# Identity transposes ahead of the first rows, and every projection one piece earlier, in a local-attention and mixture-of-experts kernel

## The chip, the cores and the metric

The kernel runs on one core of a Trainium2 chip. The time is the device time of one launch in microseconds (us); each kernel is launched several times, and the median is compared. In the code, `nc.tensor` is TensorE (PE: matrix products and transposes), `nc.vector` is VectorE (DVE), `nc.scalar` is ScalarE (ACT), `nc.gpsimd` is GpSimd (POOL), and `nc.sync` is the queue that issues the DMAs (SP).

## The reference

The input `x` has 2 sequences of 2048 rows of 256 numbers. An attention layer with 16 heads of 16, in which each row looks at itself and the 64 rows before it, is followed by a layer norm, a router that picks one of 8 experts for each row, the expert's first layer with GELU, a shared second layer, and two layer norms.

```python
qkv = x @ W_attn + b_attn
scores = jnp.einsum('bhtd,bhsd->bhts', q, k) * scale
scores = jnp.where(mask[None, None], scores, -jnp.inf)   # causal & (j >= i - 64)
attn = jax.nn.softmax(scores, axis=-1)
out = jnp.einsum('bhts,bhsd->bhtd', attn, v) ... @ W_proj + b_proj
x = _layernorm(x + out)
router_logits = x @ Wr.T
expert_idx = argmax(softmax(router_logits))
inter = gelu(x @ W1[e] + b1[e])          # e: the row's expert
y = inter @ Wo + bo + x
x = _layernorm(x + (layernorm(y) * gamma + beta))
```

## The kernel before

Everything is in 32-bit floats, apart from the masks. The 4096 rows are 32 tiles of 128 rows (`NT`), and 8 chunks of 512 rows (`CH`; 4 tiles each, `TPC`).

**Start.** SP issues the loads of the first chunk, of the bias rows `bst`, of the weights `wa` in three parts (for q, k and v) and the rest. POOL builds `ident`. PE transposes the biases into `pb` (L288) and DVE copies them to `bqkv` (L289) and scales them into `bq1` (L315); then DVE builds the masks `m_a`, `m_b` and `m_first` in some twenty small operations (L331 to L356). This part is ordered by a scheduler; from L938 on, the order of each engine's queue is the order in which the code is written.

**Projections of a chunk.** They are cut into four pieces of two parts each: piece 0 transposes the chunk's rows (L368) into `xT`, piece 1 makes q (L372), piece 2 makes k (L372), piece 3 makes v (L379). `project` issues the PE work of one part, `keep` the copies out of PSUM by ACT and DVE, `prepare` takes the buffers (and issues the load of the next chunk with piece 0, POOL's copy of 64 old columns of k with piece 2, POOL's clearing of v with piece 3). PSUM tiles of the projections come from a ring of two banks (`psum`), those of the transposes from another ring of two (`ps_t`), the scores have four banks of their own. After piece 3, DMAs shift v by 64 rows into `h` (L456 to L463). Pieces 0 to 2 of chunk 0 run ahead of the loop (L947).

**The loop over tiles** (L1000) is a hand-written software pipeline. Iteration i computes the scores of tile t = i (`scores`: masks L474, products L486), the row maxima on DVE (`row_max`, L498) and the exponentials on ACT (`exps`, L502) in four quarters, and POOL's partial sums (`fold`, L514 and L522); turns the probabilities of tile u = i-1 (`turn`, L552; copies by ACT L558 and DVE L560) and multiplies them by v (`weigh`, L572); normalises and projects tile w = i-2 (`turn_inverse` L591, `normalise` L595, `join` L603); and does the layer norm of tile z = i-3 (`norm_scale` on POOL L619 and L620, `norm` on DVE L628, `turn_x1` L641, `keep_x1` L646). Between these, iteration i does piece i % 4 of chunk i // 4 + 1. After piece 2, POOL adds the bias to the residual of the chunk (`add_bias`, L943). With i % 4 = 2 there is the router's product (`route`, L653), with i % 4 = 3 its transposition (`turn_logits`, L663, then DVE L664), once at i = 8 that of the expert biases (`turn_biases`, L933). From i = 20 on, DVE and POOL also build the lists of the rows of each expert (POOL `row` L788, i = 25 to 28). Iterations 28 to 31 have no piece.

In iteration 0, after the first quarter's maxima, the code turns the router's weights (`turn_router`, L296), makes v of chunk 0 (piece 3), and adds the bias to chunk 0's residual; the other three quarters' maxima follow on DVE. v's two additions of the bias (L446) are then ahead of them in DVE's queue.

**The experts** follow: 36 blocks of 128 gathered rows (up to 39 if the routing needs them), each a first layer (L188), GELUs (L197) and a second layer (L206).

Of the kernel before, what the change touches and what calls it, by code (L numbers as in the profile page):

```python
# [10 lines left out]
F32 = mybir.dt.float32  # L11
# [3 lines left out]
ALU = mybir.AluOpType  # L15
AX = mybir.AxisListType

P = 128
# [3 lines left out]
TPC = CH // P  # L22
NEG = -1.0e30
GAP = 64
SPLIT = (0, 16, 28, 32)
PIECES = 8
EARLY = 1
LN_EPS_BLOCK = 1e-5
LN_EPS_FFN = 1e-12
# [3 lines left out]
def kernel(  # L33
# [16 lines left out]
    nc = tc.nc  # L50
    B, T, C = x.shape
    E, _, FF = w1.shape
    KC = C // P
# [56 lines left out]
    def psum(name):  # L110
        return ps_m.tile([P, 512], F32, tag="pm", name=name)
# [136 lines left out]
    with ExitStack() as att:  # L248
# [34 lines left out]
            nc.sync.dma_start(out=bp_bc, in_=b_proj.partition_broadcast(P))  # L283


        bqkv = aw.tile([P, 3 * KC], F32, name="bqkv")
        pb = psum("pb")
        nc.tensor.transpose(pb[:, 0 : 3 * KC], bst, ident[0 : 3 * KC, 0 : 3 * KC])  # L288
        nc.vector.tensor_copy(bqkv, pb[:, 0 : 3 * KC])  # L289

        nc.gpsimd.memset(wrT, 0.0)

        def turn_router():
            pw = psum("pw")
            for k in range(KC):
                nc.tensor.transpose(pw[:, ts(k, E)], wrs[:, ts(k, P)], ident[0:E, 0:E])  # L296
            nc.vector.tensor_copy(
                wrT[:, :, 0:E], pw[:, 0 : KC * E].rearrange("p (k e) -> p k e", e=E)
            )
# [10 lines left out]
        unit = HD**-0.5 / HD  # L310
        nc.vector.tensor_scalar(half[:, 0:1], par_f, -unit, HD**-0.5, ALU.mult, ALU.add)
        nc.vector.tensor_scalar(half[:, 1:2], par_f, unit, None, ALU.mult)

        bq1 = aw.tile([P, KC], F32, name="bq1")
        nc.vector.tensor_scalar(bq1, bqkv[:, 0:KC], half[:, 1:2], None, ALU.mult)  # L315

# [35 lines left out]
        m_first = aw.tile([P, 4, P], BF16, name="m_first")  # L355
        nc.vector.tensor_copy(m_first, off.unsqueeze(1).to_broadcast([P, 4, P]))  # L356
        m_first = m_first.rearrange("p h c -> p (h c)")

        qs, ks, vs, vh, xbs, axT, x1s, x1Ts, pxs = {}, {}, {}, {}, {}, {}, {}, {}, {}
        pts, banks, probs, maxes, sums, pTs, pas, rTs, avs, norms = [{} for _ in range(10)]  # L360
# [2 lines left out]
        def project(c, piece, part):  # L363

            pm = psum(f"pj_{c}_{piece}_{part}")
            if piece == 0:
                for j in range(TPC):
                    nc.tensor.transpose(pm[:, ts(j, P)], xts[c][:, j, ts(part, P)], ident)  # L368
            elif piece in (1, 2):
                f = (piece - 1) * KC + part  # L370
                for k in range(KC):
                    nc.tensor.matmul(  # L372
                        pm, lhsT=wa[:, k, ts(f, P)], rhs=axT[c][:, k, :],
                        start=(k == 0), stop=(k == KC - 1),
                    )
            else:
                for a in range(2):
                    for k in range(KC):
                        nc.tensor.matmul(  # L379
                            pm[:, ts(a, C)],  # L380
                            lhsT=axT[c][:, k, ts(2 * part + a, P)],
                            rhs=wa[:, k, 2 * C : 3 * C],
                            start=(k == 0), stop=(k == KC - 1),
                        )
            pxs[c, piece, part] = pm

        def prepare(c, piece):

            first = c % (TPB // TPC) == 0
            if piece == 0:  # L390
                if c + 1 < B * T // CH:
                    xts[c + 1] = load_x(c + 1)
                axT[c] = p2.tile([P, KC, CH], F32, tag="xT", name=f"xT_{c}", bufs=1)
                xbs[c] = xp.tile([P, TPC, C], F32, tag="xb", name=f"xb_{c}")
            elif piece == 1:
                qs[c] = p2.tile([P, KC, 2, CH], F32, tag="q", name=f"q_{c}")
            elif piece == 2:
                ks[c] = p2.tile([P, KC, CTX + CH], F32, tag="k", name=f"k_{c}")
                if first:
                    nc.gpsimd.memset(ks[c][:, :, 0:CTX], 0.0)  # L400
                else:
                    nc.gpsimd.tensor_copy(ks[c][:, :, 0:CTX], ks[c - 1][:, :, CH : CH + CTX])
            else:

                vs[c] = p2.tile([P, TPC, NH // 2, 3, HD], F32, tag="v", name=f"v_{c}")
                nc.gpsimd.memset(vs[c][:, :, :, 1, :].rearrange("p j m d -> p (j m) d"), 0.0)

                vh[c] = p2.tile([P, TPC, NH // 2, 3, HD], F32, tag="h", name=f"h_{c}")
                if first:
                    nc.gpsimd.memset(vh[c][0:CTX, 0].rearrange("p m s d -> p (m s d)"), 0.0)  # L410
# [273 lines left out]
        def routing_constants():  # L684
            e_rank = iota([P, E], [[-1, E]], E, 0, "e_rank")[1]
            e_gap = iota([P, E], [[GAP, E]], 0, 0, "e_gap")[1]
            col = iota([P, P], [[1, P]], 0, 0, "col")
            own = iota([P, 1], [[0, 1]], 0, 1, "own")[1]
            tile1 = iota([P, NT], [[1, NT]], 1, 0, "tile1")[1]
            before = rt.tile([P, P], BF16, name="before")  # L690
            nc.gpsimd.memset(before, 1.0)
            nc.gpsimd.affine_select(
                out=before, in_=before, pattern=[[1, P]], compare_op=ALU.is_gt,
                fill=0.0, base=0, channel_multiplier=-1,
            )
            ones = rt.tile([P, P], BF16, name="ones")
            nc.gpsimd.memset(ones, 1.0)
            one_e = rt.tile([P, E], F32, name="one_e")
            nc.gpsimd.memset(one_e, 1.0)
            none = rt.tile([P, E], F32, name="none")  # L700
            nc.gpsimd.memset(none, 0.0)
            carry[-1] = none
            for n, (t0, t1) in enumerate(lots):
                pads[n] = rt.tile([P, t1 - t0 + 1, E], BF16, name=f"oh_{n}")
                nc.gpsimd.memset(pads[n][:, t1 - t0, :], 0.0)
            return e_rank, col, own, before, ones, one_e, tile1, e_gap
# [293 lines left out]
        for i in range(NT):  # L1000


            t, u, w, z = (n if n >= 0 else None for n in range(i, i - 4, -1))
            c, piece = i // TPC + 1, i % TPC
            more = c < NT // TPC
            if more:
                prepare(c, piece)
            if w is not None:
                inverse(w)
            scores(t)  # L1010
            row_max(t, 0)
            if i == 0:
                consts = routing_constants()
                turn_router()
                prepare(0, 3)
                for part in range(2):
                    project(0, 3, part)
                    keep(0, 3, part)
                add_bias(0)
            if u is not None:  # L1020
                turn(u, 0)
                keep_turned(u, 0)
                turn(u, 1)
            exps(t, 0)
            row_max(t, 1)
            if u is not None:
                keep_turned(u, 1)
            if z is not None:
                norm_scale(z)
            if more:  # L1030
                project(c, piece, 0)
            exps(t, 1)
            row_max(t, 2)
            row_max(t, 3)
            if t < NT - 1:
                fold(t, 0)
            for task in spread.get(i, ()):
                task()
            if u is not None:
                turn(u, 2)  # L1040
                keep_turned(u, 2)
                turn(u, 3)
                keep_turned(u, 3)
            if more:
                keep(c, piece, 0)
            if z is not None:
                norm(z)
            exps(t, 2)
            if more:
                project(c, piece, 1)  # L1050
            if w is not None:
                turn_inverse(w)
                normalise(w)
            if more:
                keep(c, piece, 1)
            if u is not None:
                weigh(u)
            exps(t, 3)
            if t < NT - 1:
                fold(t, 1)  # L1060
            if u is not None:
                keep_weighed(u)
            if z is not None:
                turn_x1(z)
                keep_x1(z)

            if i == TPC:
                load_experts()
            if i == 2 * TPC:
                turn_biases()  # L1070
            if i >= TPC + 3 and (i - 3) % TPC == 0:
                turn_logits((i - 3) // TPC - 1)
            for task in plan.get(i, ()):
                task()
            if w is not None:
                join(w)
            if more and piece == 2:
                add_bias(c)
            if z is not None and z % TPC == TPC - 1:
                route(z // TPC)  # L1080
# [178 lines left out]
```

## Time and profile before

| What | us |
|---|---|
| median of 3 runs (639.22 to 640.71) | 639.62 |
| the profiled execution's own time | 637.24 |
| its span, first to last instruction | 635.5 |

The loop's iterations can be read from the start of the mask products (L474) of each tile in PE's timeline:

| Iterations | start, us | length, us |
|---|---|---|
| 0 | 18.95 | scores of tile 1 begin at 26.48 and are complete only after 30.7 |
| 2 (piece 2), 3 (piece 3) | 40.52, 49.92 | 9.40, 9.71 |
| 4 (piece 0), 5 (piece 1) | 59.63, 67.99 | 8.36, 9.49 |
| 6 (piece 2, router), 7 (piece 3, logits) | 77.48, 87.55 | 10.07, 10.17 |
| 8 (piece 0, expert biases), 9 (piece 1) | 97.72, 106.86 | 9.14, 9.50 |
| 24, 25, 26, 27 (pieces 0 to 3, lists) | 251.91, 260.27, 269.76, 280.39 | 8.36, 9.49, 10.63, 10.85 |
| 28, 29, 30 (no piece) | 291.24, 299.54, 307.95 | 8.30, 8.41, 9.86 |

The profile's page gives each engine's busy share, the span in 40 slices, and the chain of work that ended last. The timeline gives instructions in order of time; a line begins with the start and the duration in us, then the engine and the line of the code, and ends, in brackets, with the time that the engine sat idle before it and what released it. A merged line's duration reaches from the first start to the last end. The view of windows gives each engine's busy time in a stretch, then the TensorE clock granted (1.00 is full), the DMA share and the rate.

### The profile page before, as it was taken

To read this page: it belongs to the slowest core of one execution; us is meant where nothing else is said; L and a number is where in the kernel's file an instruction comes from. 1 tells how busy PE (TensorE), PEld (TensorE's weight loads), DVE (VectorE), ACT (ScalarE), POOL (GpSimd) and SP (SyncE) were. 2 spreads that over 40 slices of the span, in tenths; PEclk is the share of its full clock that TensorE was granted. 3 is DMA by queue.
4 is the path that set the end of the run, shared out by engine and by line. 5 is a ranking of instruction groups with operands and counts; after the bars stand their busy time and mean duration, and the time that the engine had idled before them with its cause. 6 is when DMAs were issued, how large, how long until landed. Compare 5 with 4: busy or idle time off the path is not lost.

```text
span 635.5 us, 18444 instructions
## 1 busy us (share of the span) xinstructions
PE 575.8 (91%) x7334; PEld 467.6 (74%) x7335; DVE 382.3 (60%) x904; ACT 299.1 (47%) x997; POOL 429.0 (68%) x628
## 2 busy tenths in 40 slices
PE   5899999999999999998777993899999999999990
PEld 3467676676767767676556993799999999999990
DVE  4468877788687887988783355444434444334442
ACT  1365775766676674865743331133343333333330
POOL 4158676676867678789743487377777777777752
PEclk9889999999999999999998997799999999999995
DMA  4202503030030302004233454155555555565300
GB/s 152 74 3 51 155 9 103 19 93 20 28 79 19 101 11 67 20 11 119 78 96 131 150 168 157 50 192 183 162 172 183 205 177 163 170 186 198 119 19 16
DMA packets 34708, 65.31 MB, mean 103 GB/s; under 512 B 8555, under 2 KB 22970, under 8 KB 34620
## 3 DMA queue, kind: packets, MB, share of 16 engines
q1 hardware_dynamic: 31164, 55.19, 26.6%
q0 software_dynamic: 3456, 8.92, 5.9%
q8 instruction: 59, 0.97, 0.7%
q14 instruction: 29, 0.24, 0.1%
HBM read 49.46 MB, written 8.91 MB: 92 GB/s over the span
## 4 chain that ended last, share of the span: by engine, by line
PE 70%; POOL 11%; DVE 7%; ACT 7%; issue 4%; POOLq 0%; DVEq 0%; ACTq 0%
PE ph L188 18%; PE py L206 17%; PE pj L372 8%; ACT pr L502 5%; PE pt L552 5%; PE py L603 4%; PE pa L572 4%; PE s L486 4%; PE pj L379 3%; PE s L474 2%; POOL row L788 2%; POOL fd L522 1%; POOL fd L514 1%; PE px L641 1%; PE pr L591 1%
## 5 line engine op out<-in xcount | busy, mean ns | idle before, releaser
L197 ACT ACTIVATE gT<-ph,bc 128x128 f32<-128x128 f32 x288 | 82.4, 369 | 183.9 <-issue 155.2
L502 ACT ACTIVATE pr<-s,nm 128x128 f32<-128x128 f32 x512 | 140.7, 409 | 8.5 <-DVE nm L498 8.5
L188 PEld LDWEIGHTS ph<-xgT,wb 128*128 128x128 f32 x1152 | 134.4, 192 | 5.0 <-ACT xgT L174 1.6
L188 PE MATMUL ph<-xgT,wb 128*128 128x128 f32 x1152 | 135.2, 275 | 2.4 <-ACT xgT L174 1.3
L514 POOL TENSOR_TENSOR fd<-pr 128x512 f32<-128x512 f32 x62 | 78.7, 1271 | 78.5 <-ACT pr L502 78.4
L206 PE MATMUL py<-wo_sb,gT 128*128 128x256 f32 x576 | 131.6, 382 | 0.0
L206 PEld LDWEIGHTS py<-wo_sb,gT 128*128 128x128 f32 x576 | 107.7, 192 | 13.4
L498 DVE TENSOR_REDUCE nm<-s 128x4 f32<-128x512 f32 x128 | 82.0, 683 | 11.2 <-PE s L486 10.9
L522 POOL TENSOR_TENSOR fd<-fd 128x512 f32<-128x512 f32 (+2 forms) x93 | 76.4, 822 | 7.3
L558 ACT COPY pT<-pt 128x512 f32<-128x512 f32 x64 | 38.2, 597 | 86.0 <-DVE nm L498 53.3
L552 PE MATMUL pt<-ident,pr 128*128 128x128 f32 x512 | 71.9, 281 | 2.0 <-ACT pT L558 1.8
L552 PEld LDWEIGHTS pt<-ident,pr 128*128 128x128 f32 x512 | 57.0, 142 | 19.8 <-issue 12.5
L235 DVE TENSOR_SCALAR res<-y,mv_c,rs_c 128x256 f32<-128x256 f32 x36 | 14.9, 413 | 83.9 <-POOL rs_c L220 83.9
L372 PE MATMUL pj<-xT,wa 128*128 128x512 f32 x128 | 63.5, 625 | 1.6 <-issue 1.6
L560 DVE COPY pT<-pt 128x512 f32<-128x512 f32 x64 | 43.8, 684 | 14.3 <-PE pt L552 14.3
L219 POOL TENSOR_TENSOR rs_b<-mv_b,eps_ffn 128x1 f32<-128x1 f32 x36 | 16.0, 445 | 45.9 <-DVE mv_b L217 45.9
L486 PEld LDWEIGHTS s<-k,q 32*64 32x64 f32 x2048 | 31.5, 133 | 14.6 <-issue 14.6
L237 POOL DMA_INDIRECT out_dram<-res,s_idx_b x27 | 27.8, 1031 | 20.0 <-DVE res L235 20.0
L486 PE MATMUL s<-k,q 32*64 32x128 f32 x2048 | 39.4, 283 | 0.0
L372 PEld LDWEIGHTS pj<-xT,wa 128*128 128x128 f32 x128 | 23.4, 202 | 21.2 <-issue 20.4
L603 PE MATMUL py<-wpj,av 128*128 128x256 f32 x128 | 35.3, 399 | 2.8 <-DVE logits L664 2.1
L129 POOL DMA_INDIRECT xg<-x_d,g_idx_b x27 | 33.4, 1237 | 5.2 <-issue 5.2
(183 smaller groups left out, 830.7 us busy)
## 6 DMA issues: line engine op xcount, KB each, us to landing
wb<-in_L_ffn_W_dram SPq DMA_DIRECT2D x33, 1024.0 KB, 5.1
xt<-in_L_attn_x_dram SPq DMA_DIRECT2D x8, 512.0 KB, 5.9
x_d<-x SPq DMA_DIRECT2D x32, 128.0 KB, 1.7
h<-v SPq DMA_DIRECT2D x8, 384.0 KB, 4.5
wb<-in_L_ffn_W_dram SPq DMA_DIRECT2D x24, 128.0 KB, 2.2
h<-v SPq DMA_DIRECT2D x8, 288.0 KB, 3.3
wo_sb<-in_L_ffn_Wo_dram SPq DMA_DIRECT2D x1, 1024.0 KB, 7.0
wa<-in_L_attn_W_attn_dram SPq DMA_DIRECT2D x3, 256.0 KB, 4.5
```

The lines of the kernel that those rows point to most:

```text
L188: nc.tensor.matmul(phs[b, h][:, f % (NF // 2), :], lhsT=wb[:, k, ts(f, P)], rhs=xT[:, k, :], start=(k == 0), stop=(k == KC - 1),)
L197: nc.scalar.activation(gT[:, f, :], ph[:, f % (NF // 2), :], AF.Gelu, bias=bcs[b][:, f : f + 1], scale=1.0,)
L206: nc.tensor.matmul(py[:, 0:C], lhsT=gT[:, f, :], rhs=wo_sb[:, f, :], start=(f == 0), stop=(f == NF - 1),)
L372: nc.tensor.matmul(pm, lhsT=wa[:, k, ts(f, P)], rhs=axT[c][:, k, :], start=(k == 0), stop=(k == KC - 1),)
L486: nc.tensor.matmul(banks[i][r][a * CTX : (a + 1) * CTX, 2 * g + o, :], lhsT=qs[c][rows, g, o, t0 : t0 + CTX], rhs=ks[c][rows, g, t0 : t0 + P],
L498: nc.vector.tensor_reduce(maxes[i][:, r, :], banks[i][r], AX.X, ALU.max, negate=True)
L502: nc.scalar.activation(probs[i][:, r, x, :], banks[i][r][:, x, :], AF.Exp, bias=maxes[i][:, r, x : x + 1], scale=1.0,)
L514: nc.gpsimd.tensor_tensor(fd[:, 8 * pair : 8 * pair + 8, :], pr[:, two, :, 0:CTX].rearrange("p r x c -> p (r x) c"), pr[:, two, :, CTX:P]. ...
L522: nc.gpsimd.tensor_tensor(fd[:, :, 0:n], fd[:, :, 0:n], fd[:, :, n : 2 * n], ALU.add)
L552: nc.tensor.transpose(pt[:, x, :], probs[i][:, r, x, :], ident)
L560: nc.vector.tensor_copy(pTs[i][:, r], pt)
L603: nc.tensor.matmul(py[:, 0:C], lhsT=av[:, k, :], rhs=wpj[:, k, :], start=(k == 0), stop=(k == KC - 1),)
```

## The change

Three things. First, 16 transposes of `ident` by `ident` are issued on PE ahead of everything else, into a PSUM tile that nobody reads, and the biases' transposition with its two DVE operations is written after the masks. Secondly, iteration 0 takes all four quarters' maxima before v's biases. Thirdly, the loop does piece (i + 1) % 4 of chunk (i + 1) // 4 + 1, so that piece 0 of chunk 1 and its piece 1 both fall into iteration 0, and iteration 27 has no piece; `add_bias` follows piece 3 instead of piece 2, which is the same iteration as before; `turn_router` moves to iteration 3.

```diff
+WARM = 16
-        bqkv = aw.tile([P, 3 * KC], F32, name="bqkv")
-        pb = psum("pb")
-        nc.tensor.transpose(pb[:, 0 : 3 * KC], bst, ident[0 : 3 * KC, 0 : 3 * KC])
-        nc.vector.tensor_copy(bqkv, pb[:, 0 : 3 * KC])
...
-        bq1 = aw.tile([P, KC], F32, name="bq1")
-        nc.vector.tensor_scalar(bq1, bqkv[:, 0:KC], half[:, 1:2], None, ALU.mult)
...
         m_first = m_first.rearrange("p h c -> p (h c)")
+        pw = psum("warm")
+        for n in range(WARM):
+            nc.tensor.transpose(pw[:, 0:P], ident, ident)
+        bqkv = aw.tile([P, 3 * KC], F32, name="bqkv")
+        pb = psum("pb")
+        nc.tensor.transpose(pb[:, 0 : 3 * KC], bst, ident[0 : 3 * KC, 0 : 3 * KC])
+        nc.vector.tensor_copy(bqkv, pb[:, 0 : 3 * KC])
+        bq1 = aw.tile([P, KC], F32, name="bq1")
+        nc.vector.tensor_scalar(bq1, bqkv[:, 0:KC], half[:, 1:2], None, ALU.mult)
...
-            c, piece = i // TPC + 1, i % TPC
+            c, piece = (i + 1) // TPC + 1, (i + 1) % TPC
...
             row_max(t, 0)
             if i == 0:
                 consts = routing_constants()
+                for r in range(1, 4):
+                    row_max(t, r)
+                for r in range(2):
+                    exps(t, r)
+                prepare(0, 3)
+                prepare(1, 0)
+                for n in ((0, 3), (1, 0)):
+                    for part in range(2):
+                        project(*n, part)
+                        keep(*n, part)
+                add_bias(0)
+                for r in range(2, 4):
+                    exps(t, r)
+                for part in range(2):
+                    project(c, piece, part)
+                    keep(c, piece, part)
+                for pair in range(2):
+                    fold(t, pair)
+                continue
+            if i == 3:
                 turn_router()
-                prepare(0, 3)
-                for part in range(2):
-                    project(0, 3, part)
-                    keep(0, 3, part)
-                add_bias(0)
...
-            if more and piece == 2:
+            if more and piece == 3:
                 add_bias(c)
```

In the order of the changed kernel's queues, PE holds the 16 transposes, then `pb`, then the two parts of chunk 0's piece 0, of which the second waits for DVE (the PSUM ring of two: `warm`, `pb`, part 0, part 1); and DVE holds the whole mask chain, then `bqkv`, `bq1` and the copy of part 1.

## The prediction, as put on record before the changed kernel ran

> **What bounds the kernel now.** I read the page first, then PE's timeline at the start, in one iteration of each kind and around iteration 27, then the clock by windows.
>
> ```profile
> PE 575.8 (91%) x7334; PEld 467.6 (74%) x7335; DVE 382.3 (60%) x904; ACT 299.1 (47%) x997; POOL 429.0 (68%) x628
> ...
> PE   5899999999999999998777993899999999999990
> ...
> PE 70%; POOL 11%; DVE 7%; ACT 7%; issue 4%; POOLq 0%; DVEq 0%; ACTq 0%
> ```
>
> PE is the bound almost everywhere: in the chain that ended last it has 70% of the span. The change adds no PE work but the 16 transposes, so it can gain only where PE waits or runs slowly: the first slice, the sevens (iterations 28 to 31), and what follows.
>
> ```profile
> 5.21 1.97 PE L368 MATMUL pj<-ident,xt 128*128 128x128 f32 x8
> 5.32 0.17 DVE L289 COPY bqkv<-pb 128x6 f32<-128x6 f32 x1 [3.32 <-PE pb L288]
> 5.58 1.06 DVE L337 CAST temps<-off_i 128x128 f32<-128x128 int32 x1
> 7.99 0.69 DVE L418 COPY xT<-pj 128x512 f32<-128x512 f32 x1
> 8.77 10.34 PE L372 MATMUL pj<-xT,wa 128*128 128x512 f32 x16 [1.59 <-issue]
> ```
>
> DVE idles 3.32 us for the biases, then works on masks, so that it copies the second half of the transposed rows only at 7.99; the projections of q and k begin when that ends. They take 10.18 us until the first scores (18.95). The weight loads show why:
>
> ```profile
> 14.03 0.34 PEld L372 LDWEIGHTS pj<-xT,wa 128*128 128x128 f32 x1 [0.52 <-issue]
> 14.88 0.23 PEld L372 LDWEIGHTS pj<-xT,wa 128*128 128x128 f32 x1 [0.52 <-issue]
> 15.35 0.19 PEld L372 LDWEIGHTS pj<-xT,wa 128*128 128x128 f32 x1 [0.24 <-issue]
> ```
>
> From 8.77 on one product comes every 0.85 us, after about 14.9 every 0.43: PE starts at half its clock. (The page's clock row shows nothing of it; it knows the clock only from its first recorded change on.) The recorded changes are here:
>
> ```profile
> 25.18:28.59 3.41, 1.56 (x9) 0.61 (x7) 2.98 (x6) 2.12 (x8) 0.90 (x1) 1.00 0.58 133
> 28.59:32.00 3.41, 2.37 (x50) 1.38 (x57) 0.00 (x0) 1.57 (x7) 2.04 (x3) 0.50 0.26 68
> 32.00:35.41 3.41, 3.41 (x42) 2.56 (x27) 2.03 (x4) 1.59 (x6) 2.01 (x3) 0.50 0.01 2
> 8.11:11.53 3.42, 2.76 (x4) 1.24 (x5) 1.98 (x7) 0.00 (x0) 0.00 (x0) 1.00 0.74 243
> 11.53:14.94 3.41, 3.41 (x6) 1.34 (x5) 0.81 (x1) 0.78 (x1) 2.35 (x1) 1.00 0.00 0
> ```
>
> The clock falls at 28.59, where iteration 0 leaves PE waiting for exponentials, and comes back at 35.41, two windows of 3.41 us later. Laid backwards, the same grid has an edge at 14.94, where the products speed up. PE busy 1.56 of 3.41 us (46%) lost the clock, 2.37 (69%) and 2.76 (81%) did not bring it back, 3.41 (100%) did, twice.
>
> **What the Trainium skill says.** "TensorE: Matmul & The Clock Gate", Part 1, has this gate: half rate by default, released after a busy window of about 3.4 us, the windows running freely, so that their phase differs from launch to launch. The trace agrees on the window; on the loss, which the page puts down to an idle window, it is stricter (46% busy lost it). Part 4 of the page says that transposes do not count as PE activity. Here the window from 32.00 was filled in part by transposes (32.66 to 34.42, over half of it) and released the clock, so I take it that they count. "SBUF — State Buffer", Who interferes with whom, says that DVE's two-port copies and POOL lock each other out of a shared port; the trace agrees: `x` (L628) takes 0.33 us at least and 1.37 at most, and the mask's cast at 5.58 took 1.06 us, ending as POOL's clearings do (6.56).
>
> **The change part by part.** Sums are against the profiled execution (637.24, of which 635.5 span), 2.38 us below the median of the runs; gains are taken from that median.
>
> *Start of the projections.* The identity is there at 1.62. Eight cold transposes took 1.97 us, start to start 0.21; sixteen take 16 x 0.21 = 3.4, from 1.7 to 5.1, when the rows arrive anyway (5.21): no cost. DVE may build the masks from about 2.4 (POOL's last index pattern ends at 2.70). Their work is the 2.9 us in which DVE did them from 6.72 on (1.27 before the copy, 1.60 after), plus 0.7 for the first ones: done at 6.0 if POOL does not get in the way, 7.0 if it locks DVE out as it did at 5.58. Then come `bqkv` and `bq1`, 0.3. Now the catch: part 1 of the rows' transposes takes the bank of `pb`, so it waits for `bqkv`, which was read at 5.49 and is now read at 6.2 to 7.3; I take 6.7. Transposes to DVE's copy 1.15 (as 5.21 to 6.36), the copy 0.69, start 0.1: projections at about 8.65 instead of 8.77. Gain 0.1, from -0.6 to +0.6.
>
> *Clock in the projections.* Before, 8.77 to 14.94 is 6.17 us at half rate, 3.1 lost. Afterwards PE is busy from 1.7 to about 6 and then waits for `bqkv` and for the copy. A window can lie within 1.7 to 6, and its end releases the clock; the window after that then has PE busy for about 1.6 us of 3.41 (half of the transposes and the first products), the share at which the clock fell at 28.59. I take the case that it is lost again at the next edge and a full window of 3.41 us runs at half rate: 1.7 lost, gain 1.4. Bounds: held throughout 3.1; not released in time, 3.4 to 6.8 us cold by the phase, -0.3 to 1.4.
>
> *Iteration 0.* From the first mask product: maxima end at +4.7 (four of 0.64 to 0.69 from 21.05), v's two parts on PE at +3.9 and +5.6; DVE adds v's biases to +5.4 and +6.55, then PE transposes chunk 1 to +7.1, the copy ends at +7.95, and q's two parts take 2 x 1.73: scores of tile 1 at +11.45. Their exponentials end at +9, so they no longer hold back tile 1. Before, tile 1's scores ran as if from 30.19, +11.24: the added piece costs 0.2. Iteration 1 took from there 10.33 to 40.52, with 2.2 us of half clock in it (scores 2.01 instead of 1.21, turns 1.97 instead of 1.09, q 2.38 instead of 1.88); in the new order PE waits 0.6 and 0.9 us in iteration 0, 57% busy at worst, and I take the clock to hold: 8.1, like iteration 2 without its last tile's 1.4. Together 19.55 instead of 21.57, gain 2.0; if the clock falls all the same, 1.7 less.
>
> *The loop.* A piece moves to the neighbouring iteration, and with it meets other work:
>
> ```profile
> 65.33 0.41 PE L591 MATMUL pr<-ident,rw 128*128 128x128 f32 x2 [0.98 <-ACT pT L558]
> ...
> 105.80 1.13 PE L603 MATMUL py<-wpj,av 128*128 128x256 f32 x4 [0.32 <-DVE b1T L934]
> ...
> 305.24 0.41 PE L591 MATMUL pr<-ident,rw 128*128 128x128 f32 x2 [1.42 <-POOL rs L620]
> ```
>
> Iterations with piece 0 wait for ACT and are short (8.36). They now carry the logits, which cost piece 3 0.56 (10.17 against 9.61): the nearest row is iteration 8, where the expert biases did the same to piece 0: 9.14. DVE's copy of the rows stands ahead of the logits there, and POOL's `add_bias` (2.37) is now ahead of `rs`, so `x` may end 0.4 later, by about when PE needs it (7.1 into the iteration): I take 9.2. Piece 3 with the router costs 9.61 + 0.57. So four tiles take 9.49 + 9.49 + 10.18 + 9.2 = 38.36 instead of 38.09: -0.27 for each of five chunks, -1.35; bounds 0 and -0.4 a chunk. The expert biases meet DVE's q in iteration 8: -0.2. Iterations 2 and 3 are 9.4 + 8.6 (router's weights 0.24) instead of 19.11: +1.1. Iterations 24 to 26 hold pieces 1 to 3 instead of 0 to 2: 29.73 instead of 28.48, -1.25. Iteration 27 without a piece could be 1.9 shorter, but POOL has no gap from 277 to 305, and `rs` releases PE at 305.24; it saves only the clearing of v (0.54) and 0.3 more: +0.85 over 27 to 29. New waits on SP: the next chunk's load now waits for `add_bias` of the iteration before, with only a store of `x` behind it and four iterations to land. Sum of the loop -0.85; bounds -2 and +1.
>
> *Total:* 0.1 + 1.4 + 2.0 - 0.85 = 2.65, say 2.7: profiled execution 634.5, median 636.9.
>
> **Rivals.** (a) The clock is released early and held: gain 3.1 in the projections and 0.3 in shorter transposes, 4.7 in all: 634.9. For it: only 46% is seen to lose the clock. Against: PE's waits around 6 to 8.6. (b) The warming does not do what it says (a window needs nearly 100%, 81% was too little, and the phase is free): gain 0.5 on average, 1.8 in all, 637.8; nearly all from iteration 1. (c) Nothing to see: no clock, masks locked out by POOL (-0.6), clock lost in iteration 0 (-1.7): about 639.6. (d) Slower: in the piece-0 iterations POOL's `add_bias` makes `rs` late, its fold then locks DVE out of `x` for 1.27 us, the row copy (0.68) and the logits follow, and `join` waits at 9.15 into the iteration instead of 7.4: 10.2 instead of 9.2, six times, 6.0: 642.9. It decides from (2.7 + 1.3) / 6 = 0.7 us an iteration on. For it: `x` takes 1.30 there already. Against: in iteration 7 the same `add_bias` let `rs` end at 6.1.
>
> **How the numbers follow.** Forecast 38%, (a) 22%, (b) 20%, (c) 10%, (d) 10%. A change under 0.2% (1.3 us) can't be told from none. Faster: 37 of the forecast, 22 of (a), 15 of (b): 74%. Same: 1, 5 of (b), 10 of (c): 16%. Slower: 10%. The range runs from below (a), with both waits at their best (632.8), to (c) (639.8).
>
> **What would show it.** Right: products (L372) of chunk 0 in part 0.43 apart before 12 us; `bqkv` read after the masks and part 1 waiting for it; no clock fall between the first scores and iteration 2; iterations with i % 4 = 3 at 9.2. Wrong: projections starting well before or after 8.65; 0.85 apart until 14; iterations with i % 4 = 3 above 9.9; POOL idle before iteration 29.

## The result, and the profile after

The changed kernel took 632.38 us in the median (631.47 to 634.05), the kernel before 639.42 beside it (three of these four runs are those reported at the start): ratio 0.9891, interval 0.9861 to 0.9921. The gain is 7.0 us where 2.7 were forecast, and the time is just under the forecast range. In two later series, both on one chip, the changed kernel took 632.57 and 632.42 again, but the kernel before took 636.43 and 636.01 there (ratios 0.9931 and 0.9947), so that the gain was 3.9 and 3.6: more than forecast, and less than the first comparison says.

The profiled execution took 634.05, the slowest of its four (span 632.3). From the page, PE's busy time, the slices of PE and of the clock, and PE's share of the chain that ended last:

```profile
PE 578.3 (91%) x7351; PEld 470.5 (74%) x7351; DVE 382.6 (61%) x904; ACT 298.1 (47%) x997; POOL 425.0 (67%) x628
...
PE   8999999999999999987868993999999999999990
...
PEclk9999999999999999998898997899999999999995
...
PE 72%; POOL 10%; ACT 6%; DVE 6%; issue 4%; DMA 1%; POOLq 0%; SPq 0%; DVEq 0%; ACTq 0%
```

The first slice has risen from 5 to 8, and slices 2 and 3 of the clock from 8 to 9; the dip behind iteration 27 is no shallower (one slice at 6, where 7 was the lowest), and slices 19 and 20 now show a lower clock. The start, in the timeline (start, duration, engine, line of the changed kernel; idle time and releaser in brackets):

```profile
1.68 3.56 PE L354 MATMUL warm<-ident 128*128 128x128 f32 x16 [1.68 <-POOL ident masks.py:199]
...
5.46 1.32 PE L374 MATMUL pj<-ident,xt 128*128 128x128 f32 x8
5.57 0.43 DVE L348 CAST m_first<-temps 128x512 bf16<-128x512 f32 x1
5.91 0.16 DVE L360 COPY bqkv<-pb 128x6 f32<-128x6 f32 x1
6.12 0.42 PEld L374 LDWEIGHTS pj<-ident,xt 128*128 128x128 f32 x4 [0.25 <-DVE bqkv L360]
6.82 0.69 DVE L424 COPY xT<-pj 128x512 f32<-128x512 f32 x1
7.61 7.37 PE L378 MATMUL pj<-xT,wa 128*128 128x512 f32 x16 [0.83 <-ACT xT L422]
...
14.82 1.03 PE L480 MATMUL s<-m_first,ident_b 128*128 128x512 bf16 x4
```

The masks are done at 6.00, part 1 waits only 0.25 us for `bqkv`, and q and k take 7.2 us to the first scores instead of 10.18. PE's weight loads show the clock, one product every 0.43 us from the start:

```profile
8.12 0.19 PEld L378 LDWEIGHTS pj<-xT,wa 128*128 128x128 f32 x1 [0.24 <-issue]
8.54 0.19 PEld L378 LDWEIGHTS pj<-xT,wa 128*128 128x128 f32 x1 [0.24 <-issue]
8.97 0.19 PEld L378 LDWEIGHTS pj<-xT,wa 128*128 128x128 f32 x1 [0.24 <-issue]
```

By windows, laid on the clock's grid of 3.41 us (stretch, its length, busy time of PE, PEld, DVE, ACT and POOL with counts, then the clock):

```profile
1.59:5.00 3.41, 3.32 (x16) 3.28 (x16) 2.94 (x19) 0.50 (x1) 3.03 (x17) 1.00 0.82 221
5.00:8.42 3.42, 2.52 (x13) 1.47 (x12) 2.37 (x7) 0.59 (x1) 2.15 (x12) 1.00 1.00 301
...
277.88:281.29 3.41, 1.55 (x68) 1.14 (x66) 2.50 (x4) 3.41 (x14) 3.33 (x6) 1.00 0.02 5
281.29:284.70 3.41, 2.94 (x9) 1.74 (x11) 1.49 (x7) 0.67 (x3) 3.41 (x5) 0.53 0.16 45
284.70:288.12 3.42, 3.42 (x72) 2.25 (x72) 1.95 (x6) 0.00 (x0) 3.11 (x7) 0.50 0.39 120
```

A window filled with nothing but transposes (97% busy) released the clock, and the next one, 74% busy, kept it. (The 1.00 of the first row is no reading; the trace's record of the clock begins with full clock from 4.98 on.) Then the clock takes something back in iteration 27: PE is busy 45% of the window from 277.88, and the record has half clock from 281.5 to 288.3. (So late in the span this grid lies 0.2 us ahead of the clock's own, hence the 0.53; in the clock's own window, from 278.05, PE is busy 42%.)

Laid side by side, stage by stage (starts of mask products from PE's timeline; "again" is changed_3, the changed kernel run once more, below):

| Stage, us | before | after | again | forecast gain |
|---|---|---|---|---|
| start to first scores | 18.95 | 14.82 | 14.82 | 1.5 |
| first scores to tile 2 | 21.57 | 18.98 | 18.98 | 2.0 |
| tile 2 to tile 28 | 250.72 | 250.84 | 249.53 | -0.85 (with iterations 28 and 29) |
| tile 28 to the experts' first product | 49.00 | 52.59 | 51.43 | 0 |
| the rest of the span | 295.26 | 295.07 | 295.14 | 0 |
| span | 635.5 | 632.3 | 629.9 | 2.65 |

So the two profiles differ by only 3.2: 6.6 us are gained up to tile 28, and 3.6 are lost between there and the experts, 2.5 of them in iterations 28 to 30 (9.87, 8.41 and 10.83 us, where before they took 8.30, 8.41 and 9.86). The kernel before, in its one profile, kept its clock there.

### The profile page after: what moved, and what is told of

Read it like the earlier page. It is cut to its first block, busy times and chain, and to the rows that moved or that the text cites. A ratio compares the mean times of both kernels' runs of the same rounds, so it can differ in the third digit from the quotient of the medians.

```text
span 632.3 us, 18477 instructions
## 1 busy us (share of the span) xinstructions
PE 578.3 (91%) x7351; PEld 470.5 (74%) x7351; DVE 382.6 (61%) x904; ACT 298.1 (47%) x997; POOL 425.0 (67%) x628
## 3 DMA queue, kind: packets, MB, share of 16 engines
q1 hardware_dynamic: 31164, 55.19, 27.5%
## 4 chain that ended last, share of the span: by engine, by line
PE 72%; POOL 10%; ACT 6%; DVE 6%; issue 4%; DMA 1%; POOLq 0%; SPq 0%; DVEq 0%; ACTq 0%
PE ph L189 18%; PE py L207 17%; PE pj L378 8%; PE pt L558 5%; PE pa L578 5%; PE s L492 5%; PE py L609 4%; ACT pr L508 4%; PE pj L385 3%; PE s L480 2%; PE px L647 2%; POOL row L794 2%; PE pr L597 1%; ACT pT L564 1%; POOL fd L528 1%
## 5 line engine op out<-in xcount | busy, mean ns | idle before, releaser
L378 PE MATMUL pj<-xT,wa 128*128 128x512 f32 x128 | 60.1, 595 | 0.8 <-ACT xT L422 0.8
L220 POOL TENSOR_TENSOR rs_b<-mv_b,eps_ffn 128x1 f32<-128x1 f32 x36 | 10.1, 281 | 50.4 <-DVE mv_b L218 50.4
L227 DVE TENSOR_TENSOR y<-py,xbo 128x256 f32<-128x256 f32 x36 | 15.2, 423 | 39.6 <-PE py L207 39.5
```

The source lines that it names most:

```text
L378: nc.tensor.matmul(pm, lhsT=wa[:, k, ts(f, P)], rhs=axT[c][:, k, :], start=(k == 0), stop=(k == KC - 1),)
```

## The experiments

Each group ran on one chip with the kernel before beside it: the first four rows on one chip, the next four and the last three on a second, the rest on a third. "First scores" and "to tile 28" (from the first scores) are from the profile of one execution each. Of max_only (636.42), no_warm (638.59), no_shift_2 (632.61) and no_shift_best (625.96) that execution was the slowest or the next to it, of after_marks (624.38) the fastest.

| Kernel | median | before beside it | ratio (95%) | first scores | to tile 28 |
|---|---|---|---|---|---|
| warm_only | 635.45 | 638.76 | 0.9953 (0.9934 to 0.9972) | 15.49 | 271.84 |
| no_warm | 635.82 | 638.76 | 0.9943 (0.9927 to 0.9959) | 17.62 | 269.41 |
| loop_only | 637.04 | 638.76 | 0.9972 (0.9959 to 0.9985) | 18.54 | 270.02 |
| before_fill | 638.26 | 638.76 | 0.9991 (0.9981 to 1.0002) | 18.35 | 271.56 |
| after_again (the change) | 632.57 | 636.43 | 0.9931 (0.9908 to 0.9955) | 15.50 | 268.76 |
| after_fill | 630.07 | 636.43 | 0.9887 (0.9863 to 0.9911) | 14.82 | 268.60 |
| max_only | 633.00 | 636.43 | 0.9947 (0.9930 to 0.9964) | 18.40 | 269.25 |
| warm_1 | 633.47 | 636.43 | 0.9961 (0.9943 to 0.9978) | 16.01 | 268.94 |
| no_shift | 630.63 | 636.10 | 0.9915 (0.9892 to 0.9938) | 14.82 | 267.66 |
| after_fill_2 | 630.11 | 636.10 | 0.9915 (0.9896 to 0.9933) | 15.42 | 268.75 |
| after_marks | 627.11 | 636.10 | 0.9869 (0.9852 to 0.9887) | 14.82 | 268.56 |
| best | 625.31 | 636.10 | 0.9829 (0.9813 to 0.9845) | 14.82 | 268.75 |
| changed_3 (the change) | 632.42 | 636.01 | 0.9947 (0.9927 to 0.9966) | 14.82 | 268.51 |
| no_shift_2 | 630.90 | 636.01 | 0.9925 (0.9899 to 0.9950) | 15.21 | 267.64 |
| no_shift_best | 623.25 | 636.01 | 0.9812 (0.9791 to 0.9833) | 15.45 | 267.85 |

(The ratio is not the quotient of the two medians shown and can differ from it by a tenth of a per cent.) The kernel before takes 272.29 to tile 28, with 6.8 us of half clock in it. Up to iteration 28 before_fill is the same kernel: its row is a second profile of it.

**The start alone, the loop alone, and all but the warming.** warm_only has the first three hunks of the change (transposes, biases after the masks) and the old loop; loop_only has the old start and the new loop; no_warm is the changed kernel with this edit:

```diff
-        pw = psum("warm")
-        for n in range(WARM):
-            nc.tensor.transpose(pw[:, 0:P], ident, ident)
```

> The kernel before with only the sixteen identity transposes and the biases after the masks; the loop is that of before. Theory A (the start is worth what the profile after shows: products of q and k begin 1.1 us earlier and run 3.0 us shorter at full clock): first scores at about 14.8 us instead of 18.95, iteration 0 still loses the clock; median about 635.3, 4.1 below before. Theory B (the identities bring nothing that lasts; the gain is in the loop's new order): first scores not before 17.5, median 638 to 639.4.

> The kernel before with only the new loop (maxima first in iteration 0, every piece one iteration earlier). Theory A: no clock loss between the first scores and tile 2, which come 2.6 us closer together (19.0 instead of 21.6); the start as before; median about 637 (2.6 gained, about 0.3 lost later). Theory B: median 634 to 635, most of the 7 us.

> The changed kernel without the sixteen transposes (biases after the masks, new loop). Theory A: the products of chunk 0 come 0.85 us apart for one to two windows of 3.41 us, first scores at 16.3 to 17.8 instead of 14.82, median 2 to 3 us above the changed kernel, so 634.5 to 635.5. Theory B: within 0.5 us of the changed kernel, 632 to 633.

The start is worth 3.3 us in the median, the loop 1.7, together 5.0 on that chip; the medians of warm_only and loop_only are near those of their theories A, that of no_warm is 0.3 above its range. warm_only's first scores are 3.46 earlier, not 4.1; it still loses the clock behind iteration 0 (half clock 28.0 to 31.4), which no kernel with the new loop does.

Four profiles have the old start: in before, before_fill, loop_only and max_only q and k begin at 8.77 or 8.78 and take 10.18, 9.58, 9.77 and 9.62 us to the first scores, with full clock on record from 14.94, 13.73, 14.12 and 13.82 on. The profile that the prediction rests on is the longest of them.

no_warm is no clean comparison: the scheduler that orders the start, with the transposes gone, put the biases back ahead of the masks and the second copy of `xT` at 8.98, so that the projections went on only at 9.72 and 0.85 us apart until about 13.2.

**One transpose instead of sixteen** (`WARM = 1`) keeps DVE's order nearer to the changed one, and was to separate warming from order.

> The changed kernel with one identity transpose instead of sixteen; DVE's order is nearly that of the changed kernel, masks built while the biases are on their way, so it parts the order of DVE from the warming. Theory A (the sixteen release the clock): products of q and k begin at 7.6 to 8.4 but come 0.85 us apart for one or two windows, first scores at 16 to 17.5, median 634 to 635.5. Theory B (DVE's order is what counts): first scores below 15.3, median as the changed kernel within 0.4.

Its first products and its weight loads:

```profile
6.76 5.81 PE L378 MATMUL pj<-xT,wa 128*128 128x512 f32 x8
6.97 0.69 DVE L424 COPY xT<-pj 128x512 f32<-128x512 f32 x1
...
8.63 0.34 PEld L378 LDWEIGHTS pj<-xT,wa 128*128 128x128 f32 x1 [0.52 <-issue]
9.48 0.34 PEld L378 LDWEIGHTS pj<-xT,wa 128*128 128x128 f32 x1 [0.52 <-issue]
10.33 0.34 PEld L378 LDWEIGHTS pj<-xT,wa 128*128 128x128 f32 x1 [0.52 <-issue]
11.12 0.19 PEld L378 LDWEIGHTS pj<-xT,wa 128*128 128x128 f32 x1 [0.45 <-issue]
```

Without the warming the products are 0.85 apart until 11.1, and 0.43 afterwards. All eleven profiles of kernels with sixteen transposes have q and k at 7.2 us from their start (7.61 to 8.29) to the first scores, and full clock on record from 4.98 to 7.76 on, ahead of the first product: the clock was released and kept in each. Yet warm_1's first scores are only 0.5 to 1.2 later, and its median is 0.9 above the changed kernel's beside it, with intervals that overlap (0.9943 to 0.9978 and 0.9908 to 0.9955): between its two theories, and no proof that sixteen beat one.

The reason is that its q and k begin at 6.76, 0.85 to 1.53 earlier than with sixteen. Its rows are transposed from 4.97 on and not from 5.34 to 5.49, and its first product doesn't wait for DVE's copy (6.97 to 7.66). In the changed kernel it seems to: it starts at 7.61, right behind DVE's copy (6.82 to 7.51), while the ACT copy that its line names had ended at 6.74. So the run changes the order of the start too, and parts the two causes only roughly. Of the 2.94 us by which its first scores are earlier than in the kernel before, 2.0 are the earlier start (6.76 instead of 8.77) and 0.9 the clock, which is back after 4.3 us of products instead of 6.2. Whether the earlier work brings that, or the phase of the window in this one profile, it doesn't tell; the sixteen transposes give the clock in every profile.

**Early maxima without the shift of the pieces, with the old start** (chunk 1's piece 0 stays in iteration 0, behind v; the router's weights go to iteration 3, as in the change):

```diff
+                for r in range(1, 4):
+                    row_max(t, r)
+                for r in range(2):
+                    exps(t, r)
                 prepare(0, 3)
...
                 add_bias(0)
+                for r in range(2, 4):
+                    exps(t, r)
```

> The kernel before with the order of iteration 0 of the changed one (four maxima first, then v and piece 0 of chunk 1, router's weights in iteration 3), but every piece in its old iteration; start as before. Theory A (what iteration 1 gains is the clock, and it is piece 1 in iteration 0 that keeps PE busy enough to hold it): the clock is lost between the first scores and tile 2 as before, these two about 21 us apart; median 0 to 0.7 below before. Theory B (the early maxima let the scores of tile 1 start sooner and that is the gain): 19.5 us apart or less, median 1.5 to 2 below before.

It is worth 3.4 us in the median, although its clock fell in the scores of tile 1 (27.5 to 30.9). Tile 2 begins 18.50 us after the first scores instead of 21.57, as theory B had it. From the first scores to tile 28 it takes 3.04 less than the kernel before, of which one window less of half clock can be at most 1.7. Against before_fill, which lost one window there as max_only did, it is 2.3: so much the early maxima bring apart from the clock.

**The changed kernel without the shift** (its start and its maxima; the later pieces in their old iterations), in two series, the second beside the changed kernel:

```diff
-            c, piece = (i + 1) // TPC + 1, (i + 1) % TPC
+            c, piece = i // TPC + 1, i % TPC
...
-            if more and piece == 3:
+            if more and piece == 2:
                 add_bias(c)
```

> The changed kernel with its start (warming, biases after the masks) and with the maxima of tile 1's scores ahead in iteration 0, but with every later piece back in its old iteration (c, piece from i and not i + 1; iteration 0 then projects chunk 0's piece 3 only, and add_bias goes back to piece 2). Theory A (start about 4 us, maxima about 3, the shift of the pieces about 0.5): first scores near 15, tile 28 begins 269.2 after them instead of 268.7, and the median is 0.3 to 0.8 us above the changed kernel run beside it or on record (after/before 0.989 to 0.993), so a ratio to the kernel before near 0.992 to 0.994. Theory B (the piece ahead is what fills PE's wait in iteration 0 and keeps its clock, and its worth is hidden in the run with the old start by a lucky window): the clock is lost between the first scores and tile 2, tile 2 begins 20.5 or more after the first scores, and the ratio is 0.995 or more.

> The changed kernel once more, beside the kernel without the shift of the pieces. Both theories: first scores at 14.8 to 15.5, tile 28 268.5 to 269.0 after them where no clock is lost before it, ratio to the kernel before 0.989 to 0.993.

> The changed kernel with the later pieces in their old iterations, once more, beside the changed kernel. Theory A (the shift costs about 1.1 us, which the traces show between the first scores and tile 28, and the iterations 27 to 31 give none of it back): tile 28 267.4 to 267.9 after the first scores, and a median 0.5 to 1.7 us below the changed kernel of this call. Theory B (the shift is paid back behind tile 28, where iteration 27 is free of a piece and the clock is less often lost): the same tile 28, but a median within 0.4 us of the changed kernel's, or above it.

Both theories of the first run fell: nothing was lost by leaving the shift out. Iterations 0 and 1 in the timeline of no_shift_2, PE alone:

```profile
21.97 0.63 PE L374 MATMUL pj<-ident,xt 128*128 128x128 f32 x4 [0.50 <-DVE v L452]
22.53 0.39 PE L480 MATMUL s<-m_b,m_a 64*128 64x512 bf16 x2
23.23 0.37 PE L480 MATMUL s<-m_b,m_a 64*128 64x512 bf16 x1 [0.32 <-ACT pr L508]
24.27 0.37 PE L480 MATMUL s<-m_b,m_a 64*128 64x512 bf16 x1 [0.66 <-ACT pr L508]
...
32.24 0.61 PE L480 MATMUL s<-m_b,m_a 64*128 64x512 bf16 x4
```

and of changed_3:

```profile
21.57 0.63 PE L374 MATMUL pj<-ident,xt 128*128 128x128 f32 x4 [0.50 <-DVE v L452]
22.04 3.79 PE L378 MATMUL pj<-xT,wa 128*128 128x512 f32 x8
25.76 0.60 PE L480 MATMUL s<-m_b,m_a 64*128 64x512 bf16 x4
...
33.80 0.60 PE L480 MATMUL s<-m_b,m_a 64*128 64x512 bf16 x4
```

The piece pulled into iteration 0 (3.79 us) covers waits of 0.32 and 0.66. From the first scores, tile 2 begins after 17.03 us without the shift and 18.98 with it; the loop up to tile 28 gives back 1.08 of these 1.95. In the two profiles the shift costs 0.87 net. The medians are 1.5 us apart on the same side, as theory A had it, but the intervals of the two ratios overlap (0.9899 to 0.9950 and 0.9927 to 0.9966), so that the medians alone don't prove it. (changed_3's ratio lies above the range expected of it.)

**Transposes of the identity where PE waits in the last iterations,** from iteration 28 on in the kernel before and from 27 on in the changed one:

```diff
+            if i >= FILL_FROM:
+                pf = psum(f"fill_{i}")
+                for n in range(FILL):        # FILL = 8
+                    nc.tensor.transpose(pf[:, 0:P], ident, ident)
             if w is not None:
                 turn_inverse(w)
```

> The kernel before with eight more identity transposes (0.9 us of PE work) in each of iterations 28 to 31, in PE's 1.4 us wait ahead of turn_inverse. Theory A (the median of before stands 2.4 us above its profiled execution because most executions lose the clock once or twice among the tiles without a piece, by the phase of the window): median about 637.2, 2 us below before, and the executions closer together, no clock below 1 from 285 to 327. Theory C (the 2.4 us are something else, the clock there is as in the profile): 639.4 to 640, no better.

> The changed kernel once more, for the spread of its executions beside the others on this chip. Theory A (the start and iteration 0 are gained for good, the rest is which windows lose the clock among iterations 27 to 31): median 632 to 633, executions spread over some 3 us, spans in step with the mean clock. Theory B (the first measurement was lucky; the lasting gain is the 3.2 us by which the two profiled executions differ): median about 635.5.

> The changed kernel with eight identity transposes (0.9 us of PE work) in PE's 1.4 us wait ahead of turn_inverse in each of iterations 27 to 31. Theory A: no clock below 1 between 265 and 325, where the profile after lost 10.2 us of full clock in three windows, about 3 us of time in that execution; median 0.5 to 2 below the changed kernel (the fill of the kernel before brought 0.5). Theory C: no difference, within 0.3.

> The changed kernel with 8 transposes of the identity in each of iterations 27 to 31, once more, beside the others of this call. Theory A (they keep the clock in iterations 27 to 31 whatever the phase of the windows): no loss of clock between the first scores and the first product of the FFN, that product within 0.8 of 332.0, ratio 0.986 to 0.990. Theory B (the first run of it was a lucky phase): a loss of 3.4 us or more in iterations 27 to 31 and a ratio of 0.991 or more, as without them.

The same place of iteration 27 as above, in the windows of after_fill:

```profile
277.88:281.29 3.41, 2.43 (x76) 1.89 (x73) 2.48 (x4) 3.41 (x14) 3.33 (x6) 1.00 0.02 5
281.29:284.70 3.41, 2.91 (x61) 1.88 (x67) 2.53 (x11) 0.68 (x3) 3.41 (x5) 1.00 0.15 45
```

PE is 71% busy in this stretch instead of 45%, and the clock stays. (The clock's own windows lie elsewhere in this execution; the least busy one there, from 278.62, has PE busy for 2.21 us, 65%.) In the profiles, the five kernels with these transposes lost no clock in iterations 27 to 31; of the twelve without them nine did, 3.4 to 10.2 us of half clock in each, at different places. (after_fill lost one window behind iteration 31, from 323.0 on.) It is worth 2.5 us beside the changed kernel; the second series found the same median (630.11) and no loss at all up to the experts, but a ratio of 0.9915, over the expected 0.990 and, by itself, what theory B had. In the kernel before it brought 0.5 where more was expected, with an interval that reaches 1.0002; no execution of before_fill was above 639.8, while 7 of 38 of the kernel before beside it were above 640.

**A wait that all these kernels have.** PE's `p_tok` in the changed kernel:

```profile
395.72 0.98 PE L869 MATMUL p_tok<-marks,row 128*128 128x60 bf16 x16 [10.59 <-DVE marks L858]
```

PE waits 10.59 us for DVE's `marks`, and the clock is at half from 387.3 to 400.9, four windows, of which 5.2 us lie behind the wait. after_marks finishes DVE's list one block earlier, and best has this and the fill:

```diff
-        4: [partial(some, "others", 12)],
-        5: [partial(rest, "others"), partial(table, 1)],
+        4: [partial(rest, "others")],
+        5: [partial(table, 1)],
```

> The changed kernel with one thing more: what is left of the list 'others' (whose last operations are DVE's marks) is done in block 4 and not in block 5, where PE waits 10.6 us for the marks and afterwards runs 13.6 us at half clock in four windows. Theory A (DVE has the time in block 4, and the wait is only a matter of the order): PE's wait at p_tok falls to 2 to 6 us, half clock after it to 7 us or less, and the median is 5 to 9 us below the changed kernel: ratio 0.976 to 0.984. Theory B (DVE's work in block 4 then holds up the normalising there, and PE waits a block earlier instead): the waits of PE between 350 and 400 add up to the same within 2 us, ratio within 0.3% of the changed kernel's (0.988 to 0.994).

> Both additions to the changed kernel: 8 transposes of the identity in each of iterations 27 to 31, and the rest of 'others' in block 4. If the two are independent, its gain is the sum of what each brings over the changed kernel: about 2.5 us and 5 to 9 us, ratio 0.972 to 0.980. If the half clock after the marks comes for another reason than the wait, or the marks are as late as before, it is no better than the fill alone (0.986 to 0.990).

> Start and maxima of the change, pieces in their old iterations, 8 transposes of the identity in each of iterations 28 to 31, and the rest of 'others' in block 4. Theory A (shift costs 1.1): ratio 0.980 to 0.983, 0.5 to 1.5 us below the version with the shift (0.983). Theory B: 0.983 to 0.985, no better than it.

In after_marks:

```profile
386.25 0.98 PE L869 MATMUL p_tok<-marks,row 128*128 128x60 bf16 x16 [4.60 <-DVE marks L858]
```

The wait is 6.0 us shorter. Half clock is 6.8 us instead of 13.7 (10.2 in best), but what was saved lay in the wait: behind it there are still 4.8 us (the half clock lasts from 384.2 to 391.1), in best 7.7, where the changed kernel had 5.2. So the gain is about that of the wait; against the changed kernel's ratios of 0.9931 and 0.9947, on another chip, 0.9869 is 3.9 to 5.0 us. The ratios of after_marks and best miss their expected intervals, too high by 0.003. The combination without the shift is the fastest, 623.25, 12.8 us below the kernel before on its chip (0.9812, interval 0.9791 to 0.9833), and 2.1 below best on another chip with the same time before; the intervals overlap, but on this side, too, the version without the shift is the faster one.

## Why the prediction was wrong

*The step that failed: "Clock in the projections".* I took it that a window with half its time busy would lose the clock again, and counted 1.4. What failed is the busy time of that window, put at 1.6 us: it was 2.52 us, 74%, because `bqkv` was read at 5.91 and not at 6.7, so that part 1 of the rows waited only 0.25 us, and the products began at 7.61 and not at 8.65. The clock held: 10.18 less 7.21, 2.97 (2.4 to 2.6 against the other three profiles with the old start). In all eleven profiles with sixteen transposes the window behind the release was 72 to 85% busy. That a share of 47% loses the clock was right: no window below 48% kept it in any profile. The mechanism of rival (a) was the right one, and its 3.1 the right bound. I had put a share on a stretch whose busy time I had myself estimated.

*"Start of the projections"*: forecast 0.1, measured 1.16 here, 0.5 in after_again. The chain (masks, `bqkv`, part 1) is as described; the masks came out at the early end of the interval that I gave, and in the first profile the rows' eight transposes ran at full clock (1.32 us instead of 1.97), which depends on where the window's edge falls: after_again has 1.97 again, and starts 0.68 later. That the sixteen transposes cost nothing was not quite so: the rows were transposed from 5.46 on, and from 4.97 in warm_1. The two steps together brought 4.13 us in this profile, where 1.5 were forecast.

*"Iteration 0"*: 2.6 instead of 2.0, to scores of tile 1 at +10.94 (forecast +11.45) and 8.04 for iteration 1 (8.1). But I had the added piece cost 0.2; it costs 1.95, and the early maxima, with the clock that they keep, gain 4.54 (21.57 to 17.03 in no_shift). Of that gain the kernel before's two windows of half clock can be at most 3.4.

*"The loop"*: forecast -0.85, measured +1.19 to tile 28 in changed_3 (-0.12 in the first profile, which lost the clock in iteration 27). Iterations with piece 0 and logits took 9.01 instead of 9.2, those with piece 3 and router 10.09 instead of 10.18, so a chunk takes 38.09 as before: from tile 4 to tile 24 the -1.35 and -0.2 came out at -0.13. Iterations 24 to 26 cost 0.85 instead of 1.25; iterations 2 and 3 gave the 1.1, and iteration 27 1.04. But the +0.85 was forecast for iterations 27 to 29 together, and there changed_3 lost 1.96, as its clock fell twice; after_again, which kept it, gained 0.63. A clock lost behind iteration 27 was not in the sum at all. Added piece and loop together were forecast at -1.05 and came out at -0.87: the two errors cancel, the sign of the shift was right.

*The basis.* I took the sum from one profiled execution of the kernel before, whose clock held in iterations 28 to 31, and the gain from the median, 2.4 above it. What is lost from there to the experts differs by up to 3.2 us between executions of one kernel (tile 28 to the experts' first product is 52.59, 51.43 and 49.43 in three profiles of the change). The kernel before's own median was 639.4 in the first comparison and 638.8, 636.4, 636.1 and 636.0 in the later series. The granted clock explains that only in part: at the same mean clock its executions took 0.6 to 2.4 us longer on the chip with 638.8 than on the two others. The changed kernel's three medians lie within 0.2, but two of them are of one chip. Why the kernel before was slower in the first comparison stays open, and with it why the gain was 7.0 there and 3.6 and 3.9 in two others. The difference of the two single spans, 5.6 with changed_3, lies between.

Rival (d) did not happen: POOL's `add_bias` cost the piece-0 iterations nothing that shows. Rival (b) fell with the first weight loads. The sum of rival (c) does not come out as written: 2.65 less 1.4, 0.7 and 1.7 is -1.15, hence 640.8 and not 639.6; only the upper end of the range rests on it.

"TensorE: Matmul & The Clock Gate" in the Trainium skill, Part 4, does not count transposes as activity; the window from 1.59, 97% transposes, released the clock, so here they count, as read before from 32.00; in all eleven profiles with sixteen of them the clock was full before PE had done any product. (The profile lists them as MATMUL; whether they run in the transpose mode that the page means, no run here shows.) Part 1's windows, free in phase, agree with the 3.41 us between edges, and with edges at 4.98 and 7.76 in two executions of the changed kernel.

## What to carry to other kernels

Read the share of PE's busy time in each window of the clock before costing a wait: in these 17 profiles no window with PE over 57% busy lost the clock, and none below 48% kept it. So waits of 1.5 us and more in a window of 3.41 us could cost one to three windows at half clock, up to 1.7 us each, and a few transposes of data already there kept it. When a change bundles three parts, price and run them apart: two gained here, and the third, by its two profiles, lost a part of it. Take a ledger by stages from more than one execution, for stages near such a threshold vary by microseconds.

## What the runs showed of the hardware that was not expected

A wait of 10.6 us on PE brought four windows at half clock (13.7 us; five, 17.1 us, in after_again, behind 10.9), one of 4.6 us two or three (6.8, 10.2), part of them inside the wait.

Keeping the clock takes less than getting it back. Counted over the clock's own windows in all 17 profiles, it fell only behind windows in which PE was busy for 57% or less (the busiest: 1.94 of 3.41 us in max_only, from 24.06), while sixteen windows that were no busier kept it (the lowest: 1.68 us, 49%, in after_fill, from 329.81). It came back behind windows 84% (2.88 us in max_only, from 399.53) to 100% busy, but one of 91% (3.12 us in after, from 281.46) did not bring it back. Neither limit is sharp in these figures; the ends of matmuls are modelled, and some records may be missing.

Sixteen transposes of the identity took 3.68 us at half clock, and 3.56 where the clock came back during the last of them; eight at full clock took 1.04.
